# A selective scan in units of one channel chunk by four states, with B's product on TensorE and GpSimd for the last image

## The chip, the cores and the metric

The kernel runs on one core of a Trainium2 chip. Its engines are called by the names of the profile: PE (TensorE), DVE (VectorE), ACT (ScalarE), POOL (GpSimd) and SP (SyncE, which issues most DMAs here). The metric is the device time of one execution in microseconds (us); lower is better. Before the change the median of three runs was 25,891.06 us (25,885.81 to 25,894.32).

## The reference

Two layers work on x of shape (4, 128, 128, 128): four images of 128 x 128 pixels and 128 channels, all float32. Each layer adds its result to its input, after a group norm.

- Layer 0 is a deformable convolution in two groups of 64 channels. A convolution gives an offset for each of nine taps; at each displaced place the input is sampled bilinearly from four neighbours; a depthwise 3 x 3 convolution and a 1 x 1 convolution follow.
- Layer 1 takes each image row as four rows of 128 tokens in blocks, and runs two Mamba blocks over them. The heart of a block, per channel d (256 of them) and state n (16):

```python
deltaA = jnp.exp(jnp.einsum('btd,dn->btdn', delta, A))
deltaBu = jnp.einsum('btd,btn->btdn', delta * u, Bm)
...
    h = dA * h + dBu
    y = jnp.einsum('bdn,bn->bd', h, c)
```

delta comes from a softplus, B and C from a projection of u, and after the scan `y + u * Dp` is multiplied by silu(res) and projected. The group norm of layer 1 takes statistics over a whole image of layer 0's result, so layer 1 of an image begins when layer 0 of it is done.

## The kernel before

Layer 0 of image 0 runs alone. Then layer 1 of image b runs beside layer 0 of image b + 1, and layer 1 of the last image runs alone. The two are written as Python generators, `layer0` and `layer1`, and the loop at the end of `block_kernel` (L732 to L745) takes steps of each in turn: 512 steps of layer 1 for an image, and 289 of layer 0, of which the last falls 24 steps before the image's end. The framework places instructions on the engines' queues and makes all waits; each engine runs its queue in order.

Layer 0, by step: `gather` (L347) issues eight indirect DMAs from POOL's queue, of 128 rows each, into two of four `gt` buffers; that is, two steps are in flight. `sample` (L368) multiplies them by the bilinear weights, the first half in one DVE product (`gw`, L387), the second in sixteen ACT instructions (L382), PE transposes the sums into PSUM, and ACT copies them into one of NSB = 4 buffers `s` (L401). `add_up` (L404) applies the combined convolutions on PE. `table_part` (L207) builds the table that is gathered from: it loads four rows and one more into `xt` (two buffers), normalizes them into `xg` (one buffer) and writes eight DMAs of 64 KB. All tables are built before layer 1 starts.

Layer 1, by job: a job is one block of four image rows (TB = 512 tokens, SR = 4 sequences of 128) in one of the two Mamba layers; there are 64 jobs for an image. `pre` (L511) makes u, the gate g, delta, B and C of the next job, in pieces between the units of the job before it: a projection with u on PE, softplus from Abs, Relu, Exp and Ln on ACT and three DVE operations (L588 to L590), and `du` = delta * u (L591). B and C are written to DRAM (`bcd`) and read back, broadcast to 128 partitions.

`main` (L598) has eight units for a job. A unit covers both channel chunks (NC = 2, 128 channels each) and NQ = 2 states: a tile of 128 x 2,048.

- Loads of B and of C, 512 KB each, two buffers of each (L617).
- ACT: a zero copy into the first column of each sequence (L622) and four exponentials (L627) into one of three `da` buffers.
- DVE, images 0 to 2: two products du * B of 128 x 1,024 into `hs` (L661), one scan over 2,048 (L667), one product with C (L670). The products are `scalar_tensor_tensor` with a column of ones.
- DVE, last image: four scans of 512 that read B's product from PSUM (L653), and one `tensor_tensor` with C (L656). B's product is made from a transposed du (`turn_du`, L496): xs = dut * B, for one state of the two on POOL (L646), for the other on ACT (L644), then PE transposes it back into PSUM (L651).
- PE adds the sixteen transposed 128 x 128 blocks into `y` (L674, in the helper at L128). `y` is opened by the products with D (L606).

After eight units y is multiplied by the gate (L677), transposed, projected, and either becomes the next layer's input or is written out (L676 to L702).

Of the kernel before, what the change touches and what calls it, by code (L numbers as in the profile page):

```python
# [31 lines left out]
XP = DTR + 1 + 2 * NS  # L32

# [30 lines left out]
def block_kernel(ctx: ExitStack, tc: tile.TileContext, a: dict, out: bass.AP):  # L64
# [26 lines left out]
    pb = ctx.enter_context(tc.tile_pool(name="l0b", bufs=1))  # L91
    ps = ctx.enter_context(tc.tile_pool(name="l0ps", bufs=2, space=PSUM))
    psa = ctx.enter_context(tc.tile_pool(name="l0psa", bufs=2, space=PSUM))
# [3 lines left out]
    psy = ctx.enter_context(tc.tile_pool(name="l1psy", bufs=1, space=PSUM))  # L97

# [6 lines left out]
    offw = loadw("offw", [P, NT, 64])  # L105
# [10 lines left out]
    ones = cw.tile([P, P], F32, name="ones")  # L116
    nc.vector.memset(ones, 1.0)

    wc = cw.tile([P, NT, NT, CG], F32, name="wc")
# [43 lines left out]
    cvw = loadw("cvw", [P, NL, DCONV, NC * P], pool=p2, tag="hs")  # L163
# [7 lines left out]
    xn = cw.tile([P, RB + 2, WP], F32, name="xn")  # L171
    nc.vector.memset(xn, 0.0)

    NSB = 4
    sbuf_s = [cw.tile([P, 4, WP], F32, name=f"s{i}") for i in range(NSB)]
# [5 lines left out]
    def stats_part(b, j):  # L181
        if j == 0:
            stats[b] = small.tile([P, NJ, 6], F32, tag="stats", name=f"stats_{b}")
        xr = pb.tile([P, 4, P], F32, tag="xr", name=f"xr_{b}_{j}", bufs=2)
        nc.sync.dma_start(xr, x[b, 4 * j : 4 * j + 4].rearrange("r w c -> w r c"))
        pt4 = ps.tile([P, 4, P], F32, tag="t", name=f"pt4_{b}_{j}")
        for i in range(4):
            nc.tensor.transpose(pt4[:, i, :], xr[:, i, :], ident)
        nc.vector.bn_stats(stats[b][:, j, :], pt4.rearrange("p r w -> p (r w)"))

    def norm_part(b):
# [3 lines left out]
        for nm, v in (("s", scale), ("b", bias)):  # L195
# [4 lines left out]
            row = small.tile([P, P], F32, tag=f"row_{nm}", name=f"row_{nm}_{b}")  # L200
# [6 lines left out]
    def table_part(b, j):  # L207
# [4 lines left out]
        xt = pb.tile([P, 5, P], F32, tag="xt", name=f"xt_{b}_{j}", bufs=2)  # L212
# [4 lines left out]
        xg = pb.tile([P, G, 5, CG], F32, tag="xg", name=f"xg_{b}_{j}", bufs=1)  # L217
# [248 lines left out]

    NDA = 3
    das = [cw.tile([P, NC, NQ, SR, P], F32, name=f"da{i}") for i in range(NDA)]
    zero = cw.tile([P, NC * NQ * SR], F32, name="zero")
    nc.vector.memset(zero, 0.0)  # L470
    n_da = [0]

# [20 lines left out]
    duts = []  # L493
    n_dut = [0]

    def turn_du(st, nm):  # L496

        if not duts:
            duts.append(p2.tile([P, 2, SR, NC * P], F32, tag="hs", name="duts"))
        n_dut[0] += 1  # L500
        dut = duts[0][:, n_dut[0] % 2]
        for k in range(SR // 2):
            pt = ps1.tile([P, 2, NC, P], F32, tag="t", name=f"pdu_{nm}_{k}")
            for i in range(2):
                for c in range(NC):
                    o = (2 * k + i) * P
                    nc.tensor.transpose(pt[:, i, c, :], st["du"][:, c, o : o + P], ident)
            nc.scalar.copy(dut[:, 2 * k : 2 * k + 2], pt.rearrange("p s c d -> p s (c d)"))  # L508
        st["dut"] = dut

    def pre(st, l):  # L511

        blk = st["blk"]
        nm = f"{blk}_{l}"
# [45 lines left out]
        if in_last(blk):  # L560

            pbt = ps1.tile([P, SR, XP], F32, tag="t", name=f"pbt_{nm}")
            for i in range(SR):
                nc.tensor.transpose(pbt[:, i, :], dbl[:, i * P : (i + 1) * P], ident[0:XP, 0:XP])
            st["bt"] = p2.tile([P, SR, NS], F32, tag="bt", name=f"bt_{nm}", bufs=2)
            nc.scalar.copy(st["bt"], pbt[:, :, DTR + 1 : DTR + 1 + NS])
# [4 lines left out]
        du = p2.tile([P, NC, TB], F32, tag="du", name=f"du_{nm}", bufs=2)  # L571
# [11 lines left out]
        nc.scalar.activation(du, w1, AF.Ln)  # L583
        nc.scalar.activation(w1, w1, AF.Identity, bias=-1.0)
# [3 lines left out]
        nc.vector.tensor_tensor(e, w1, e, ALU.subtract)  # L588
        nc.vector.tensor_tensor(de, de, e, ALU.subtract)
        nc.vector.tensor_tensor(de, de, du, ALU.add)  # L590
        nc.vector.tensor_tensor(du, de, u, ALU.mult)  # L591
        st.update(u=u, g=g, delta=de, du=du, bcd=bcd)
        st.pop("dut", None)
        if in_last(blk) and duts:
            yield
            turn_du(st, nm)

    def main(st, l):  # L598

        blk = st["blk"]  # L600
        nm = f"{blk}_{l}"

        y = psy.tile([P, SR, NC, P], F32, tag="y", name=f"y_{nm}")
# [6 lines left out]
        if in_last(blk) and "dut" not in st:  # L610
            turn_du(st, nm)
        for q in range(NS // NQ):
            bc = []
            for w in range(in_last(blk), 2):
                t = p2.tile([P, NQ, TB], F32, tag=f"bc{w}", name=f"bc{w}_{nm}_{q}", bufs=2)
                n0 = w * NS + q * NQ
                nc.sync.dma_start(t, st["bcd"][n0 : n0 + NQ, :].partition_broadcast(P))  # L617
                bc.append(t)
            da = das[n_da[0] % NDA]
            n_da[0] += 1  # L620

            nc.scalar.copy(da.rearrange("p c n s t -> p (c n s) t")[:, :, 0], zero)  # L622
            for c in range(NC):
                dv = st["delta"][:, c].rearrange("p (s t) -> p s t", s=SR)
                for n in range(NQ):
                    s = q * NQ + n
                    nc.scalar.activation(  # L627
                        da[:, c, n, :, 1:], dv[:, :, 1:], AF.Exp, scale=aneg[:, l, c, s : s + 1]
                    )
            dc = da.rearrange("p c n s t -> p c (n s t)")  # L630
            cv = bc[-1].rearrange("p n t -> p (n t)").unsqueeze(1).to_broadcast([P, NC, NQ * TB])
            if in_last(blk):


                for n in range(NQ):
                    s = q * NQ + n

                    xs = (p2 if n else pb).tile(
                        [P, SR, NC * P], F32, tag="bc0" if n else "gw", name=f"xs_{nm}_{s}", bufs=2
                    )  # L640
                    for i in range(SR):
                        bv = st["bt"][:, i, s : s + 1]
                        if n:
                            nc.scalar.activation(xs[:, i], st["dut"][:, i], AF.Copy, scale=bv)  # L644
                        else:
                            nc.gpsimd.tensor_scalar(xs[:, i], st["dut"][:, i], bv, None, ALU.mult)  # L646
                    for c in range(NC):
                        pool, tag = (ps, "t") if n else (psa, "acc")
                        px = pool.tile([P, SR, P], F32, tag=tag, name=f"px_{nm}_{s}_{c}")
                        for i in range(SR):  # L650
                            nc.tensor.transpose(px[:, i, :], xs[:, i, c * P : (c + 1) * P], ident)  # L651
                        dn = da[:, c, n].rearrange("p s t -> p (s t)")
                        nc.vector.tensor_tensor_scan(  # L653
# [57 lines left out]
    def layer1():  # L711
        for _ in pre(*jobs[0]):
            pass
# [30 lines left out]
    for _ in l1:  # L744
        pass  # L745
# [77 lines left out]
```

## Time and profile before

The profiled execution has a span of 24,903.2 us from the first to the last instruction, with a mean granted PE clock of 0.905. Its own time is known by this span alone; the median of the runs is 987.9 us above it.

| Stage (us from the span's start) | length | PE busy | DVE busy | ACT busy | POOL busy | DMA share | GB/s |
|---|---|---|---|---|---|---|---|
| 0 to 275: statistics and table of image 0 | 275 | 55 | 98 | 7 | 1 | 0.51 | 147 |
| 275 to 3,344: layer 0 of image 0, other tables | 3,069 | 2,494 | 686 | 1,373 | 2,335 | 0.50 | 144 |
| 3,344 to 20,567: layer 1 of images 0 to 2, layer 0 of 1 to 3 | 17,223 | 13,966 | 16,346 | 11,257 | 13,270 | 0.48 | 156 |
| 20,567 to 24,903: layer 1 of the last image | 4,337 | 3,471 | 3,805 | 3,471 | 2,350 | 0.21 | 69 |

Busy times are in us. In the page's groups of instructions, a line names the code line, the engine, the operation, the tiles written and read, their shapes and the count; then the busy time of the group and the mean of one in ns; then the idle time of the engine just before these instructions and what ended most of it. In a timeline, a line is a start and a length in us, the engine, line, operation and tiles, and in brackets the idle time before. A line of waits names who waited, for whom, the sum in us, how often, and the longest.

Of rows that the diff touches: the scan of 2,048 (L667) takes 4,422 ns, the product of 2,048 with C 2,350 ns (L670, scalar_tensor_tensor) or 2,289 ns (L656, tensor_tensor), a scan of 512 from PSUM 1,202 ns, an exponential 711 ns on ACT, and one xs on POOL 1,164 ns on average.

### The profile page before, as it was taken

The numbers are of one execution on the slowest core, as the hardware profiler recorded it, in microseconds if no ns is written. First come the engines' busy times: TensorE is split into PE (matmuls) and PEld (weight loads), VectorE is DVE, ScalarE is ACT, GpSimd is POOL, SyncE is SP. The second block draws the span as 40 slices with busy tenths as digits, with TensorE's granted clock in tenths as the row PEclk, the third lists the DMA queues.
The fourth block names the chain that finished last, engine by engine and source line by source line (L and its number), as shares of the span: only waits on it lengthen the run. The fifth ranks groups of instructions, "written<-read, shape, count | busy, mean of one in ns | idle before, by whom it ended". The sixth has DMA issues, their size and how long they took to land. (4 is left out here: it accounts for less than half of the span.)

```text
span 24903.2 us, 331178 instructions
## 1 busy us (share of the span) xinstructions
PE 19986.7 (80%) x121156; PEld 13946.7 (56%) x121156; DVE 20935.3 (84%) x13018; ACT 16107.7 (65%) x38037; POOL 17956.4 (72%) x11270
## 2 busy tenths in 40 slices
PE   5788788888888878888888878888888877878877
PEld 3555455555555555555555555555555556666666
DVE  2221269999999999999999999999999998888888
ACT  2444466666666666666666666666666667888887
POOL 4777777887887857788887866787887845555555
PEclk8999989999999888999999888999999889999999
DMA  4554544454444444454544444454454442222221
GB/s 136 157 159 130 151 142 157 156 161 158 158 159 156 158 145 153 157 162 157 159 161 155 159 150 151 153 163 158 159 160 157 157 138 67 69 69 71 70 69 68
DMA packets 1530815, 3471.82 MB, mean 139 GB/s; under 512 B 243283, under 2 KB 717651, under 8 KB 1529052
## 3 DMA queue, kind: packets, MB, share of 16 engines
q1 hardware_dynamic: 1086812, 2242.08, 28.0%
q0 software_dynamic: 442368, 1208.55, 15.4%
q8 instruction: 951, 15.58, 0.3%
q14 instruction: 684, 5.60, 0.1%
HBM read 3299.19 MB, written 150.47 MB: 139 GB/s over the span
## 5 line engine op out<-in xcount | busy, mean ns | idle before, releaser
L359 POOL DMA_INDIRECT gt<-table,idx x9216 | 15606.0, 1693 | 4665.8 <-issue 2582.2
L627 ACT ACTIVATE da<-de,aneg 128x508 f32<-128x508 f32 x8192 | 5455.4, 711 | 2609.2 <-PE y L128 2357.7
L667 DVE TENSOR_TENSOR_SCAN da<-da,hs 128x2048 f32<-128x2048 f32 x1536 | 6792.2, 4422 | 120.2 <-ACT da L627 23.8
L128 PE MATMUL y<-ident,da 128*128 128x128 f32 x32768 | 4753.9, 306 | 2176.1 <-DVE da L670 1901.2
L420 PE MATMUL acc<-s,wc 128*64 128x256 f32 (+3 forms) x38400 | 6060.3, 439 | 276.7 <-ACT s L401 269.1
L128 PEld LDWEIGHTS y<-ident,da 128*128 128x128 f32 x32768 | 4247.0, 159 | 2997.4 <-DVE da L670 2050.8
L382 ACT ACTIVATE gw<-gt,wt 128x64 f32<-128x64 f32 x18432 | 4613.2, 337 | 1024.2 <-DMA gt<-table,idx 592.1
L420 PEld LDWEIGHTS acc<-s,wc 128*64 128x64 f32 x38400 | 3200.8, 140 | 2440.1 <-issue 1287.5
L128 PE MATMUL p<-ident,gw 128*128 128x128 f32 x18432 | 2896.6, 305 | 1471.5 <-DVE gw L387 1215.5
L646 POOL TENSOR_SCALAR xs<-duts,bt 128x256 f32<-128x256 f32 x2048 | 2349.7, 1164 | 2249.2 <-ACT duts L508 1185.7
L661 DVE SCALAR_TENSOR_TENSOR hs<-du,ones,bc 128x1024 f32<-128x1024 f32 x3072 | 3828.0, 1281 | 0.0
L670 DVE SCALAR_TENSOR_TENSOR da<-da,ones,bc 128x2048 f32<-128x2048 f32 x1536 | 3609.6, 2350 | 31.8
L128 PEld LDWEIGHTS p<-ident,gw 128*128 128x128 f32 x18432 | 2363.9, 157 | 2272.0 <-DVE gw L387 1150.1
L387 DVE TENSOR_TENSOR gw<-gt,wt 128x1024 f32<-128x1024 f32 x1152 | 1403.7, 1219 | 2357.9 <-DMA gt<-table,idx 1883.7
L653 DVE TENSOR_TENSOR_SCAN da<-da,px 128x512 f32<-128x512 f32 x2048 | 2350.6, 1202 | 509.2 <-PE px L651 509.2
L401 ACT COPY s<-p 128x512 f32<-128x512 f32 x1152 | 669.7, 581 | 2102.5 <-PE p L128 2100.1
L530 PE MATMUL pu<-hp,inc 128*128 128x512 f32 x4096 | 1830.4, 594 | 1.1 <-ACT ot L700 0.8
L651 PE MATMUL px<-ident,xs 128*128 128x128 f32 x8192 | 1213.5, 287 | 537.8 <-DVE da L653 322.1
L651 PEld LDWEIGHTS px<-ident,xs 128*128 128x128 f32 x8192 | 972.2, 147 | 818.0 <-POOL xs L646 329.3
L530 PEld LDWEIGHTS pu<-hp,inc 128*128 128x128 f32 x4096 | 747.8, 190 | 813.1 <-issue 809.3
L656 DVE TENSOR_TENSOR da<-da,bc 128x2048 f32<-128x2048 f32 x512 | 1172.0, 2289 | 6.6
L644 ACT ACTIVATE xs<-duts,bt 128x256 f32<-128x256 f32 x2048 | 894.3, 499 | 19.3 <-PE px L651 18.8
(133 smaller groups left out, 14768.7 us busy)
## 6 DMA issues: line engine op xcount, KB each, us to landing
bc<-bcd SPq DMA_DIRECT2D x3584, 512.0 KB
gt<-table,idx POOLq DMA_INDIRECT x9216
table<-xg SPq DMA_DIRECT2D x1016, 64.0 KB
xt<-in_x SPq DMA_DIRECT2D x124, 320.0 KB
xr<-in_x SPq DMA_DIRECT2D x128, 256.0 KB
x<-xo SPq DMA_DIRECT2D x128, 256.0 KB
x1t<-x SPq DMA_DIRECT2D x128, 256.0 KB
x1t_o<-x SPq DMA_DIRECT2D x128, 256.0 KB
```

Source lines behind the costliest of these rows:

```text
L128: nc.tensor.matmul(o, v, ident, is_transpose=True, start=start, stop=stop, skip_group_check=True)
L359: nc.gpsimd.indirect_dma_start(out=gt[:, v, r], out_offset=None, in_=flat, in_offset=bass.IndirectOffsetOnAxis(ap=idx[:, ri, o : o + 1], a ...
L382: nc.scalar.activation(gw[:, r, s, v], gts[h][:, v, r, s * CG : (s + 1) * CG], AF.Copy, scale=wt[:, u, r0 + r, s, v : v + 1],)
L420: nc.tensor.matmul(accs[b, j + i0][CG * g : CG * g + CG, q : q + rb - ra, :], wc[sl, v, e, :], st[p + 4 * g if p < 4 else 8][sl, ra:rb, kx ...
L530: nc.tensor.matmul(px.rearrange("p (s t) -> p s t", s=SR), inc[:, l, j, c * P : (c + 1) * P], h[:, :, j : j + P], start=(j == 0), stop=(j ...
L627: nc.scalar.activation(da[:, c, n, :, 1:], dv[:, :, 1:], AF.Exp, scale=aneg[:, l, c, s : s + 1])
L646: nc.gpsimd.tensor_scalar(xs[:, i], st["dut"][:, i], bv, None, ALU.mult)
L651: nc.tensor.transpose(px[:, i, :], xs[:, i, c * P : (c + 1) * P], ident)
L653: nc.vector.tensor_tensor_scan(dn, dn, px.rearrange("p s t -> p (s t)"), 0.0, ALU.mult, ALU.add)
L661: nc.vector.scalar_tensor_tensor(hs[:, :, n, :], st["du"], ones[:, 0:1], bc[0][:, n].unsqueeze(1).to_broadcast([P, NC, TB]), op0=ALU.mult, ...
L667: nc.vector.tensor_tensor_scan(df, df, hs.rearrange("p c n t -> p (c n t)"), 0.0, ALU.mult, ALU.add)
L670: nc.vector.scalar_tensor_tensor(dc, dc, ones[:, 0:1], cv, op0=ALU.mult, op1=ALU.mult)
```

## The change

A unit is now one channel chunk by NU = 4 states, still 128 x 2,048, and there are still eight for a job. In all images B's product of a unit has one source:

- Images 0 to 2: one DVE product of 2,048 (du of the chunk, broadcast over the states, times B), one scan, one product with C. B and C of four states, 1 MB each, are loaded every second unit. `du` has one buffer and is made during the last unit of the job before.
- Last image, chunk 0: du is transposed in a permuted order, so that 32 tokens of each of four groups lie on 32 partitions. `make_d` (POOL) spreads B over a 32-column mask, and `fill` makes the product B * du on PE in sixteen matmuls of 32 rows, straight into a PSUM tile of four banks.
- Last image, chunk 1: `times_b` multiplies du by the broadcast B on POOL, 128 x 2,048.
- Last image: the exponentials of a unit are issued two units ahead, into four `da` buffers whose first columns are zeroed once; the scan writes into its own `he` buffers (three).
- Layer 0's tiles lie in pools of their own, which are released before the last image; those used only while image 0 is alone, in one released before layer 1. `xt` has four buffers, `xg` two, `s` three (NSB).
- The softplus: w1 - 1 - e is one scalar_tensor_tensor; an ACT instruction falls away.

```diff
+QW = P // SR
+NU = 4
...
-    NSB = 4
-    sbuf_s = [cw.tile([P, 4, WP], F32, name=f"s{i}") for i in range(NSB)]
+    NSB = 3
+    sbuf_s = [l0w.tile([P, 4, WP], F32, name=f"s{i}") for i in range(NSB)]
...
-        xt = pb.tile([P, 5, P], F32, tag="xt", name=f"xt_{b}_{j}", bufs=2)
+        xt = pp.tile([P, 5, P], F32, tag="xt", name=f"xt_{b}_{j}", bufs=4)
...
-        xg = pb.tile([P, G, 5, CG], F32, tag="xg", name=f"xg_{b}_{j}", bufs=1)
+        xg = pp.tile([P, G, 5, CG], F32, tag="xg", name=f"xg_{b}_{j}", bufs=2)
...
+    def load_bc(st, u):
+
+        bc = []
+        for w in range(2):
+            t = lm["pool"].tile([P, NU, TB], F32, tag=f"bc{w}", name=f"bc{w}_{st['nm']}_{u}", bufs=2)
+            n0 = w * NS + u * NU
+            nc.sync.dma_start(t, st["bcd"][n0 : n0 + NU, :].partition_broadcast(P))
+            bc.append(t)
+        st["bc", u] = bc
...
-        nc.scalar.activation(w1, w1, AF.Identity, bias=-1.0)
...
-        nc.vector.tensor_tensor(e, w1, e, ALU.subtract)
+        nc.vector.scalar_tensor_tensor(e, w1, -1.0, e, op0=ALU.add, op1=ALU.subtract)
...
+    def make_du(st):
+
+        du = p2.tile([P, NC, TB], F32, tag="du", name=f"du_{st['nm']}")
+        nc.vector.tensor_tensor(du, st["delta"], st["u"], ALU.mult)
+        st["du"] = du
...
+    def main(st, l, nst, nl):
...
+        for k in range(NC * NS // NU):
+            u, c = divmod(k, NC)
+            if c == 0:
+                load_bc(st, u)
+            bt, ct = (t.rearrange("p n t -> p (n t)") for t in st["bc", u])
...
+            hs = lm["pool"].tile([P, NU, TB], F32, tag="hs", name=f"hs_{nm}_{k}")
+            nc.vector.scalar_tensor_tensor(
+                hs, st["du"][:, c].unsqueeze(1).to_broadcast([P, NU, TB]), one, st["bc", u][0],
+                op0=ALU.mult, op1=ALU.mult,
+            )
+            if k == NC * NS // NU - 1 and nst and not in_last(nst["blk"]):
+                make_du(nst)
+            df = da.rearrange("p n s t -> p (n s t)")
+            nc.vector.tensor_tensor_scan(df, df, hs.rearrange("p n t -> p (n t)"), 0.0, ALU.mult, ALU.add)
+            nc.vector.scalar_tensor_tensor(df, df, one, ct, op0=ALU.mult, op1=ALU.mult)
...
-                for n in range(NQ):
-                    nc.vector.scalar_tensor_tensor(
-                        hs[:, :, n, :], st["du"], ones[:, 0:1],
-                        bc[0][:, n].unsqueeze(1).to_broadcast([P, NC, TB]),
-                        op0=ALU.mult, op1=ALU.mult,
-                    )
...
+    def make_d(st, u):
+
+        d = le["r"].tile([P, SR, NU, QW], F32, tag="D", name=f"D_{st['nm']}_{u}", bufs=3)
+        nc.gpsimd.tensor_tensor(
+            d, st["bt"][:, :, NU * u : NU * u + NU].unsqueeze(3).to_broadcast([P, SR, NU, QW]),
+            le["mask"].unsqueeze(1).unsqueeze(1).to_broadcast([P, SR, NU, QW]), ALU.mult,
+        )
+        st["D", u] = d
+
+    def fill(st, u):
+
+        px = le["ps"].tile([P, SR, NU, P], F32, tag="dbu", name=f"px_{st['nm']}_{u}")
+        for q in range(SR):
+            for g in range(SR):
+                o = slice(g * QW, (g + 1) * QW)
+                nc.tensor.matmul(
+                    px[:, g, :, q * QW : (q + 1) * QW],
+                    st["dut"][o, q], st["D", u][o, q],
+                    start=True, stop=True, skip_group_check=True,
+                )
+        st["px"] = px
+
+    def times_b(st, u):
+
+        t = le["r"].tile([P, SR, NU, P], F32, tag="dbu", name=f"dbu_{st['nm']}_{u}", bufs=2)
+        nc.gpsimd.tensor_tensor(
+            t, st["du1"].rearrange("p (s t) -> p s t", s=SR).unsqueeze(2).to_broadcast([P, SR, NU, P]),
+            st["bc", u][0].rearrange("p n (s t) -> p s n t", s=SR), ALU.mult,
+        )
+        st["dbu", u] = t
+
+    def main_last(st, l, nst, nl):
...
+        for k in range(nk):
+            u, c = divmod(k, NC)
+            nxt = (st, u + 1) if k + 2 < nk else (nst, 0)
+            if nxt[0]:
+                if c == 0:
+                    load_bc(*nxt)
+                    if k + 2 < nk:
+                        make_d(*nxt)
+                else:
+                    times_b(*nxt)
+            if k + 2 < nk:
+                exps(st, l, k + 2)
+            elif nst:
+                exps(nst, nl, k + 2 - nk)
+            hs = le["r"].tile([P, SR, NU, P], F32, tag="he", name=f"he_{nm}_{k}", bufs=3)
+            src = st.pop(("dbu", u)) if c else st["px"]
+            nc.vector.tensor_tensor_scan(
+                hs.rearrange("p s n t -> p (s n t)"),
+                st.pop(("da", k)).rearrange("p s n t -> p (s n t)"),
+                src.rearrange("p s n t -> p (s n t)"), 0.0, ALU.mult, ALU.add,
+            )
+            if c == 0 and nxt[0]:
+                fill(*nxt)
+            nc.vector.tensor_tensor(
+                hs, hs, st["bc", u][1].rearrange("p n (s t) -> p s n t", s=SR), ALU.mult
+            )
```

## The prediction

> **What bounds the kernel now.** I read the 40 slices first, then the groups by line, then the timelines of VectorE (DVE) and GpSimd (POOL) side by side, then the waits. The slices show three stages: a start without scans (to 3,344 us), 1,536 scan units of images 0 to 2 beside the gathers (to 20,567 us), and the last image without gathers (4,337 us).
>
> ```profile
> DVE  2221269999999999999999999999999998888888
> POOL 4777777887887857788887866787887845555555
> ...
> L359 POOL DMA_INDIRECT gt<-table,idx x9216 | 15606.0, 1693 | 4665.8 <-issue 2582.2
> L667 DVE TENSOR_TENSOR_SCAN da<-da,hs 128x2048 f32<-128x2048 f32 x1536 | 6792.2, 4422 | 120.2 <-ACT da L627 23.8
> L661 DVE SCALAR_TENSOR_TENSOR hs<-du,ones,bc 128x1024 f32<-128x1024 f32 x3072 | 3828.0, 1281 | 0.0
> L670 DVE SCALAR_TENSOR_TENSOR da<-da,ones,bc 128x2048 f32<-128x2048 f32 x1536 | 3609.6, 2350 | 31.8
> ```
>
> In the middle DVE is busy 16,346 of 17,223 us: it sets the pace, and 565 us of its idle time are waits of gw (L387) for gathered rows. POOL, which only issues gathers there, looks like a cover (13,270 us busy). One plain unit shows how thin that cover is:
>
> ```profile
> 12083.29 4.42 DVE L667 TENSOR_TENSOR_SCAN da<-da,hs 128x2048 f32<-128x2048 f32 x1
> 12087.75 2.35 DVE L670 SCALAR_TENSOR_TENSOR da<-da,ones,bc 128x2048 f32<-128x2048 f32 x1
> 12090.02 2.48 DVE L661 SCALAR_TENSOR_TENSOR hs<-du,ones,bc 128x1024 f32<-128x1024 f32 x2
> 12092.60 4.42 DVE L667 TENSOR_TENSOR_SCAN da<-da,hs 128x2048 f32<-128x2048 f32 x1
> ```
>
> ```profile
> 12084.42 4.05 POOL L359 DMA_INDIRECT gt<-table,idx  x1 [0.30 <-ACT da L627]
> 12088.78 2.15 POOL L359 DMA_INDIRECT gt<-table,idx  x1 [0.31 <-issue]
> 12091.23 0.95 POOL L359 DMA_INDIRECT gt<-table,idx  x1 [0.30 <-issue]
> 12092.48 0.95 POOL L359 DMA_INDIRECT gt<-table,idx  x1 [0.30 <-issue]
> ```
>
> A gather takes 0.95 us if it finds DVE between two operations. Issued inside the scan it ends 0.76 us after the scan does (12,088.47 against 12,087.71); issued inside the C product, 0.83 us after that. So a DVE operation with two SBUF inputs holds POOL's read until it ends, and POOL gets in at each boundary. This unit of 9.31 us has four: after the scan, after the C product, between the two hs products, and after the second.
>
> POOL's own waits in the steady part (4,000 to 20,400 us) are its whole reserve:
>
> ```profile
> POOL gt L359 <- DVE gw L387: 1144.2, 151, 112.1
> POOL gt L359 <- ACT gw L382: 376.9, 94, 27.1
> ```
>
> With smaller ones they come to 1,590 us; the rest of the 16,400 us is 6,609 gathers at 1.93 us and 0.3 us of issue.
>
> The last image runs at 4,337 / 64 = 67.8 us a job (one block, one layer, eight units); DVE is busy 3,805 / 64 = 59.5 us of it. Its large wait is L653 for px, 509 us in all, where POOL, ScalarE and TensorE pass xs on.
>
> ```profile
> 22566.71 2.29 DVE L656 TENSOR_TENSOR da<-da,bc 128x2048 f32<-128x2048 f32 x1
> 22568.92 4.55 DVE L653 TENSOR_TENSOR_SCAN da<-da,px 128x512 f32<-128x512 f32 x4
> ```
>
> ```profile
> 22563.30 3.62 POOL L646 TENSOR_SCALAR xs<-duts,bt 128x256 f32<-128x256 f32 x4 [11.69 <-PE px L651]
> 22567.15 5.34 POOL L646 TENSOR_SCALAR xs<-duts,bt 128x256 f32<-128x256 f32 x4 [0.23 <-PE px L651]
> ```
>
> Beside scans that read PSUM, four xs take 3.62 us (0.92 us each alone, counted over 1,300); those that meet the two-input C product take 5.34.
>
> **Start.** xg gets two buffers, xt four. A table step takes 5.7 us now; DVE waits for the table writes before refilling xg (91.9 us in 30 waits until 340 us). SP's own issue of a step is 8 x 0.455 + 0.43 = 4.1 us, the next limit: 30 x 1.6 = -48 us. If the transfers bind, 0. Afterwards POOL is 76% busy and 22% issuing (2,335 and 668 of 3,069 us): nothing more to win.
>
> **Middle, DVE.** Two hs products of 1,024 become one of 2,048. Their pair spans 2.48 us; a 2,048 product (L670) takes 2.35: -0.13 us a unit, at most -0.20 if the 0.12 us before the scan shrinks to the 0.04 us that stand between scan and product. 1,536 x 0.13 = -200 us (-130 to -310). Scan, C product, exponentials, transposes and loaded bytes per unit stay. du is multiplied later, once as before; e as scalar_tensor_tensor costs 256 x 0.06 = 16 us, inside the rounding.
>
> **Middle, POOL.** This is where I choose. The boundary between the two hs products disappears. A gather started 1.1 us after the C product now waits for the end of hs, ends 0.82 us later, and the next starts about 1 us into the scan: three gathers in 9.2 us (3.07 us each) instead of four in 9.31. Counted in the instruction records of the steady part, 1,087 gathers got their read at this boundary; so many must be fitted elsewhere. POOL's 1,590 us hold 1,590 / 3.07 = 518 of them, if every wait can be used. The other 569 run only while DVE stands idle, at 0.95 + 0.30 = 1.25 us: +711 us, entered as gw waiting for its gather. Gaps at image changes (up to 112 us) can't be used, so I take +750. Upper bound 1,150: most of the waits remain. Lower bound 350: half of the losses are recovered at the ends of other operations (gw, softplus and g products) or fall where POOL has time.
>
> In sentences apart: the Trainium skill, "SBUF — State Buffer" (Who interferes with whom), says that a DVE instruction with two SBUF inputs and a GpSimd instruction that reads SBUF exclude each other for the whole instruction, whichever is first. The 4.05 and 0.95 us rows agree for short POOL reads, and it speaks against making DVE instructions longer here. By the busy shares alone the middle would be -200 us; by rows and rule it is +550.
>
> **Last image, DVE.** Four 512 scans (4.58 us) and a C product (2.21 from start to next start) become one 2,048 scan (4.46, as L667) and the same product: 13.34 us for the chunk 0 and chunk 1 units. Four pairs are 53.4; softplus, du and g products (some five of 1.2 us) add 5.9: 59.3 us. Exponentials and the first px are made a unit or more ahead; I leave 1 us of waits: 60.3 us, -480 us over 64 jobs.
>
> **Last image, POOL.** New rows: times_b, 2,048 elements from two SBUF inputs, and make_d, 512, once a pair. Near rows: in xs, a C product begun 0.22 us after it lasted 2.39 instead of 2.27 us, one begun 0.44 us after was not lengthened. So 256 elements of one input are read within 0.2 to 0.34 us; two inputs in turn give 3.2 to 5.4 us for times_b and 0.8 to 1.36 for make_d. times_b waits for the chunk 1 scan that frees its buffer, is held by that unit's C product, then reads beside the chunk 0 scan, which has one SBUF input: 4.46 us hide it. make_d, queued behind times_b, comes next, at the end of the C product, and holds up the chunk 1 scan. I take 4.2 us (hidden) and 1.05 us (paid): 4.2 us a job, so 64.5 us, -210 us (-480 without any holding; +110 at 5.4 and 1.36). If the whole 0.92 us scaled with length (7.35 and 1.84), 4.7 us a pair are paid: +730.
>
> "GPSIMD Engine Reference" (Performance versus the Vector engine) gives 4,497 ns for a 2,048-element fp32 tensor_tensor; with that the sum is the same. No run here shows it yet.
>
> **Other waits.** px has one buffer: fill waits for the chunk 0 scan, TensorE's y transposes queue behind it; 16 small matmuls, priced by L606's 0.13 us spacing at 2 to 4 us, have 9 us until the next chunk 0 scan. B and C loads double to 1 MB every second unit: a C load waits on SP two units ahead, the gather stage's loads queue behind it, and DVE has some 18 us before it needs it. In the last image the rate goes from 69 to about 140 GB/s, below the middle's 156. Three s buffers: TensorE's own order has used the first pair before the third's copy; were it not so, 864 copies of 0.58 us would be 500 us. ScalarE loses xs and the zero copies there. All at nothing.
>
> **Sum.** -48 - 200 + 750 - 210 = +292 us. Made on the profiled span: 24,903 + 292 = 25,195. Of what lies around the span I only know that the median is 988 us above it; I keep that: 25,891 + 292 = 26,183, taken as 26,180 us (1.1% slower). If that part scaled, it would change by 12 us.
>
> **Rivals.**
> - POOL's reserve is enough (faster): its 24% idle and issue time speaks for it, DVE's existing gw waits and the three-in-9.2 count against. Then -48 - 200 - 210: 25,433 us.
> - The gathers bind, but DVE is not held in the last image: -48 + 550 - 480 = +22: 25,913 us. The lengthened 2.39 us products speak against.
> - times_b reads longer than the chunk 0 scan (from 4.46 us on), at the whole xs price: 25,891 - 48 + 550 + 730 = 27,123 us. The short read found in xs speaks against.
>
> **Numbers.** Forecast 0.60, rivals 0.22, 0.11, 0.07. The forecast's own range is 25,700 to 26,650; with 8 in 10 it reaches down to the first rival: 25,430 to 26,650. About 0.2% (52 us) can be told from no change: faster 0.25 (the first rival, and a little of the second), same 0.07, slower 0.68.
>
> **What would show it.** Gathers of the plain middle units: three a unit, their mean up from 1.93 towards 2.3 us; gw's waits up from 565 to some 1,300 us and POOL's waits for gw nearly gone; the middle some 550 us longer. In the last image a job near 64.5 us, make_d ending about 1 us after a C product and the scan behind it late. I am wrong if gathers still go four to a unit, or if gw's waits stay: then the first rival holds.

## The result and the profile after

| | before | after |
|---|---|---|
| median of the timed runs, us | 25,892.69 (25,885.81 to 25,933.18, 4 runs) | 26,847.44 (26,817.57 to 26,882.69, 4 runs) |
| ratio | | 1.0367, 95% interval 1.0353 to 1.0382 |
| profiled span, us | 24,903.2 | 26,880.9 |
| start, to the first main scan | 3,344 | 4,304 |
| middle, to the end of the last main scan | 17,218 | 17,976 |
| last image | 4,341 | 4,600 |

The change costs 955 us, 3.7%. The forecast had the sign, and 1.1%; the time lies outside its range of 25,700 to 26,650 us.

The two spans can't be subtracted: 960 of their 1,978 us lie in the start. The first experiment shows that this part is not the change's. What is the change's stands in the two other stages: +758 and +259 us.

From the page of the changed kernel, the two slices that were shown of before (busy tenths of VectorE and GpSimd) and the groups that answer to those of before (line, engine, operation; busy us and mean ns; idle time ahead of them and what ended most of it):

```profile
DVE  2211115889888889988998899988899899999998
POOL 3555557888888886888888886888888864444444
...
L365 POOL DMA_INDIRECT gt<-table,idx x9216 | 17443.0, 1893 | 4550.8 <-issue 2639.4
L696 DVE TENSOR_TENSOR_SCAN da<-da,hs 128x2048 f32<-128x2048 f32 x1536 | 6792.1, 4422 | 303.8 <-ACT da L687 174.4
L697 DVE SCALAR_TENSOR_TENSOR da<-da,one,bc 128x2048 f32<-128x2048 f32 x1536 | 3614.7, 2353 | 34.1
L689 DVE SCALAR_TENSOR_TENSOR hs<-du,one,bc 128x2048 f32<-128x2048 f32 x1536 | 3614.5, 2353 | 0.0
L740 POOL TENSOR_TENSOR dbu<-du,bc 128x2048 f32<-128x2048 f32 x256 | 1420.8, 5562 | 1713.7 <-issue 944.5
L778 DVE TENSOR_TENSOR he<-he,bc 128x2048 f32<-128x2048 f32 x512 | 1565.1, 3076 | 2.2
```

VectorE's product with B is cheaper, as meant: 3,614.5 us where two products were 3,828.0. In the middle many of VectorE's nines have become eights all the same: it is busy 16,162 of 17,976 us, against 16,343 of 17,218. It does 181 us less and stands idle 939 us more. The gathers became longer, 1,893 ns on average from 1,693, and VectorE's C product of the last image lasts 3,076 ns where it lasted 2,289.

A plain stretch of the middle like the one shown of before, first VectorE, then GpSimd, in the changed kernel (start, duration, engine, line, operation):

```profile
12102.14 4.42 DVE L696 TENSOR_TENSOR_SCAN da<-da,hs 128x2048 f32<-128x2048 f32 x1
12106.60 2.35 DVE L697 SCALAR_TENSOR_TENSOR da<-da,one,bc 128x2048 f32<-128x2048 f32 x1
12108.87 2.35 DVE L689 SCALAR_TENSOR_TENSOR hs<-du,one,bc 128x2048 f32<-128x2048 f32 x1
12111.32 4.42 DVE L696 TENSOR_TENSOR_SCAN da<-da,hs 128x2048 f32<-128x2048 f32 x1
```

```profile
12103.23 4.09 POOL L365 DMA_INDIRECT gt<-table,idx  x1 [0.30 <-issue]
12107.63 2.15 POOL L365 DMA_INDIRECT gt<-table,idx  x1 [0.30 <-issue]
12110.08 1.96 POOL L365 DMA_INDIRECT gt<-table,idx  x1 [0.30 <-issue]
12112.34 4.16 POOL L365 DMA_INDIRECT gt<-table,idx  x1 [0.30 <-issue]
```

Three gathers to a unit, each ending after a VectorE operation has ended: 12,107.32 after the scan (12,106.56), 12,109.78 after the C product (12,108.95), 12,112.04 after the product with B (12,111.22). Between 5,000 and 20,000 us there are 456 units that take less than 10 us from one scan's start to the next, and so hold no other large operation of VectorE; in 438 of them exactly three gathers begin (mean 2.91). In the kernel before there are 533, and four gathers begin in 448 of them (mean 3.60). These plain units are counted in the same way below. The price of the lost gather, in the waits of the middle of the changed kernel (us in total, times, longest):

```profile
DVE gw L393 <- DMA gt<-table,idx: 1101.5, 244, 10.2
DVE da L696 <- ACT da L687: 174.4, 67, 9.1
...
POOL gt L365 <- DVE gw L393: 462.6, 58, 94.5
```

gw waits 1,102 us for gathered rows (565 before), and GpSimd's own waits for gw, its reserve, fell to 463 us. In the middle of the kernel before, as profiled in experiment 1, they were:

```profile
POOL gt L359 <- DVE gw L387: 1216.7, 165, 112.1
```

The last image, VectorE, GpSimd and TensorE in one stretch of the changed kernel:

```profile
24024.68 4.41 DVE L771 TENSOR_TENSOR_SCAN he<-da,px 128x2048 f32<-128x2048 f32 x1
24029.01 4.42 DVE L771 TENSOR_TENSOR_SCAN he<-da,dbu 128x2048 f32<-128x2048 f32 x1
24033.35 8.79 DVE L778 TENSOR_TENSOR he<-he,bc 128x2048 f32<-128x2048 f32 x2
24045.26 4.42 DVE L771 TENSOR_TENSOR_SCAN he<-dae,px 128x2048 f32<-128x2048 f32 x1 [3.13 <-PE px L730]
```

```profile
24033.51 6.48 POOL L740 TENSOR_TENSOR dbu<-du,bc 128x2048 f32<-128x2048 f32 x1 [4.37 <-DVE he L771]
```

```profile
24036.24 2.03 PE L579 MATMUL pr<-w_resw,hp 128*128 128x256 f32 x4 [2.17 <-ACT u L574]
24038.19 1.22 PE L730 MATMUL px<-D,dut 32*128 32x128 f32 x12
24041.49 2.08 PE L579 MATMUL pr<-w_resw,hp 128*128 128x256 f32 x4 [2.07 <-ACT u L574]
24043.49 1.65 PE L730 MATMUL px<-D,dut 32*128 32x128 f32 x20
```

Here VectorE does not run scan, C, scan, C, as the code has it: it does both scans of the pair and then both C products. So it goes in 129 of the 256 pairs, two in each job. GpSimd's product (times_b), freed at the end of the chunk 1 scan, waits through the first C product (2.26 us in the instruction records), takes its turn at the boundary, and the second C product, issued at 24,035.53, lasts 6.60 us in place of 2.28. In one of the two pairs of each job a C product is held like that, 64 times, 276 us in all. In the other, both C products last some 3.1 us beside make_d; 161 C products are held so, 127 us in all, and 34 chunk 1 scans last 5.26 us in place of 4.41, 29 us. Then VectorE waits 3.13 us for px, whose filling TensorE has in two pieces behind the residual products (pr) of the next job, and these wait for ScalarE. The second C product ends at 24,042.14 and the filling at 24,045.14: the hold and the filling run side by side, and the filling is the later by 3 us.

### The profile page after: what moved, and what is told of

Same layout as the page of the kernel before. It is cut to its first block, busy times and chain, and to the rows that moved or that the text cites. A ratio compares the mean times of both kernels' runs of the same rounds, so it can differ in the third digit from the quotient of the medians.

```text
span 26880.9 us, 317133 instructions
## 1 busy us (share of the span) xinstructions
PE 20386.5 (76%) x120900; PEld 13857.4 (52%) x120900; DVE 21108.1 (79%) x10014; ACT 14999.2 (56%) x35223; POOL 19595.9 (73%) x9734
## 4 chain that ended last, share of the span: by engine, by line
POOL 32%; issue 21%; DVE 17%; PE 15%; ACT 7%; DMA 4%; another core or an unknown queue 3%; SPq 0%; DVEq 0%; ACTq 0%; POOLq 0%
POOL gt L365 32%; PE acc L426 6%; DVE he L771 5%; DMA gt<-table,idx 4%; DVE da L696 4%; PE p L134 2%; DVE da L697 2%; ACT gw L388 2%; DVE hs L689 2%; PE y L134 2%; DVE he L778 2%; ACT da L687 1%; DVE gw L393 1%; PE pr L579 1%
## 5 line engine op out<-in xcount | busy, mean ns | idle before, releaser
L365 POOL DMA_INDIRECT gt<-table,idx x9216 | 17443.0, 1893 | 4550.8 <-issue 2639.4
L687 ACT ACTIVATE da<-de,aneg 128x508 f32<-128x508 f32 x6144 | 4081.1, 711 | 1449.8 <-PE y L134 1373.9
L134 PE MATMUL y<-ident,da 128*128 128x128 f32 x24576 | 3591.6, 306 | 1591.6 <-DVE da L697 1570.5
L134 PEld LDWEIGHTS y<-ident,da 128*128 128x128 f32 x24576 | 3197.5, 159 | 2342.3 <-DVE da L697 1721.1
L697 DVE SCALAR_TENSOR_TENSOR da<-da,one,bc 128x2048 f32<-128x2048 f32 x1536 | 3614.7, 2353 | 34.1
L689 DVE SCALAR_TENSOR_TENSOR hs<-du,one,bc 128x2048 f32<-128x2048 f32 x1536 | 3614.5, 2353 | 0.0
L740 POOL TENSOR_TENSOR dbu<-du,bc 128x2048 f32<-128x2048 f32 x256 | 1420.8, 5562 | 1713.7 <-issue 944.5
L134 PE MATMUL y<-ident,he 128*128 128x128 f32 x8192 | 1369.0, 334 | 797.9 <-DVE he L778 797.9
L134 PEld LDWEIGHTS y<-ident,he 128*128 128x128 f32 x8192 | 1209.1, 176 | 971.9 <-DVE he L778 851.5
L778 DVE TENSOR_TENSOR he<-he,bc 128x2048 f32<-128x2048 f32 x512 | 1565.1, 3076 | 2.2
```

Of the source, the lines that this page charges most:

```text
L134: nc.tensor.matmul(o, v, ident, is_transpose=True, start=start, stop=stop, skip_group_check=True)
L365: nc.gpsimd.indirect_dma_start(out=gt[:, v, r], out_offset=None, in_=flat, in_offset=bass.IndirectOffsetOnAxis(ap=idx[:, ri, o : o + 1], a ...
L687: nc.scalar.activation(da[:, i, :, 1:], dv[:, :, 1:], AF.Exp, scale=aneg[:, l, c, n : n + 1])
L689: nc.vector.scalar_tensor_tensor(hs, st["du"][:, c].unsqueeze(1).to_broadcast([P, NU, TB]), one, st["bc", u][0], op0=ALU.mult, op1=ALU.mult,)
L697: nc.vector.scalar_tensor_tensor(df, df, one, ct, op0=ALU.mult, op1=ALU.mult)
L740: nc.gpsimd.tensor_tensor(t, st["du1"].rearrange("p (s t) -> p s t", s=SR).unsqueeze(2).to_broadcast([P, SR, NU, P]), st["bc", u][0].rearr ...
```

## The experiments

Edits are against the changed kernel unless said otherwise. Stages are read as above; the two figures of the changed kernel to compare with are 17,976 us (middle) and 4,600 us (last image).

**1. The kernel before, profiled again.** No edit.

> The kernel before, unchanged, profiled a second time, because its first profile (span 24,903 us) lies 988 us under the median of its timed runs (25,891), while the changed kernel's profile (span 26,881) lies at its timed runs. Between the two profiles the start (up to the first 2,048-element scan of the main loop) went from 3,344 to 4,304 us, the middle from 17,223 to 17,981, the last image from 4,321 to 4,594. Theory A: the start of the kernel before also takes about 4,300 us in most of its executions, and the first profile caught a short one: span about 25,890, start about 4,330, middle 17,220 and last image 4,320 as before. Then the changed kernel's loss is 758 + 273, less some 30 to 70 at the start. Theory B: the start is 3,344 us in every execution, and the 988 us lie in the middle or the last image of the timed runs: span about 25,890 with the start at 3,344; then the changed kernel has lost 960 us in the start by itself and won elsewhere.

Span 25,822.5 us: start 4,257, middle 17,224, last image 4,341. Theory A holds. Runs 2 to 4, made together with this one, show the same start (4,256, 4,218 and 4,213 us), and the seven runs made in two later groups (5 to 8 and 9 to 11), all of edited versions of the changed kernel, have 3,303 to 3,319 us, while the timed median of the kernel before was 25,808 us in the first group and 24,911 and 24,891 in the later ones. So the start takes one of two lengths some 900 us apart, the same for all runs made together, in both kernels alike; why, these runs don't show. Within the first group the start of the edited versions of the changed kernel is 39 to 44 us shorter than before's.

**2. One product with B in the kernel before.**

```diff
-                for n in range(NQ):
-                    nc.vector.scalar_tensor_tensor(
-                        hs[:, :, n, :], st["du"], ones[:, 0:1],
-                        bc[0][:, n].unsqueeze(1).to_broadcast([P, NC, TB]),
-                        op0=ALU.mult, op1=ALU.mult,
-                    )
+                nc.vector.tensor_tensor(
+                    hs, st["du"].unsqueeze(2).to_broadcast([P, NC, NQ, TB]),
+                    bc[0].unsqueeze(1).to_broadcast([P, NC, NQ, TB]), ALU.mult,
+                )
```

> The kernel before with the product with B of the main loop as one tensor_tensor of 2,048 elements for both states and chunks, instead of two of 1,024; all else as it was, the last image too. Theory A (the boundary between the two products let a fourth gather of each unit read its indices): VectorE's own work in the middle falls by some 150 to 230 us, the mean gather rises from 1.93 to 2.1 to 2.3 us, and the middle grows from 17,223 us to between 17,700 and 18,100. Rival (the loss in the middle comes with something else of the change: the loads of 8 KB a partition, three s buffers in place of four, the units of one chunk): the middle stays at 17,223 or falls, down to 17,000, with the mean gather within 0.1 us of 1.93.

Ratio 1.037 (1.0350 to 1.0391): this one edit costs as much as the whole change. Middle 18,153 us, VectorE busy 16,067 (277 less, where 150 to 230 were expected) and idle 2,086 (1,206 more); 2.92 gathers to a plain unit; mean gather 2.21 us. Theory A; the middle grew by 50 us more than its upper bound. The last image is unchanged at 4,341.

**3. The product with B cut in two in the changed kernel.**

```diff
-            nc.vector.scalar_tensor_tensor(
-                hs, st["du"][:, c].unsqueeze(1).to_broadcast([P, NU, TB]), one, st["bc", u][0],
-                op0=ALU.mult, op1=ALU.mult,
-            )
+            for i in range(0, NU, 2):
+                nc.vector.scalar_tensor_tensor(
+                    hs[:, i : i + 2], st["du"][:, c].unsqueeze(1).to_broadcast([P, 2, TB]), one,
+                    st["bc", u][0][:, i : i + 2], op0=ALU.mult, op1=ALU.mult,
+                )
```

> The changed kernel with the main loop's product with B cut into two instructions of 1,024 elements, two states each; the units, the loads, the buffers and the last image stay as changed. Theory A (the missing boundary): the mean gather falls from 2.17 to about 1.9 us, the middle from 17,981 us to between 17,000 and 17,350, and the whole by 600 to 950 us, to 25,900 to 26,250. Rival (other parts of the change hold the middle): the two products cost 2.48 us in place of 2.35, which is some 200 us more of VectorE's work over 1,536 units, and the middle stays within 200 us of 17,981.

Ratio 1.0022 (1.0012 to 1.0031), where the changed kernel has 1.0367. Middle 17,026 us, 3.78 gathers to a plain unit, last image 4,597. VectorE does 180 us more and idles 1,129 us less. VectorE's largest wait in the middle of this kernel, against the 1,101.5 above:

```profile
DVE gw L393 <- DMA gt<-table,idx: 286.6, 84, 7.7
```

So the missing boundary holds the whole loss of the middle, and the rest of the change had won 198 us there (17,224 to 17,026, at the same busy time of VectorE). Which part of it won them was not tried.

**4. and 5. The hold in the last image.** In the first attempt a one-element copy on GpSimd read the end of the C product ahead of times_b, but into a tile of its own; in the second it writes into the tile that times_b then fills. The second edit:

```diff
-                else:
-                    times_b(*nxt)
...
+            if c and nxt[0]:
+                times_b(*nxt, hs[:, SR - 1, NU - 1, P - 1 :])
...
+        if gate is not None:
+            nc.gpsimd.tensor_copy(t[:, SR - 1, NU - 1, P - 1 :], gate)
```

> The changed kernel with GpSimd's product with B of the last image (chunk 1) issued behind a one-element GpSimd copy that reads the end of the C product of chunk 1, so that it starts beside the next scan of chunk 0, which reads PSUM, and not as soon as the scan that frees its buffer ends. In the changed kernel 64 C products of the last image, one a job, last 6.6 us where others last 2.28, and 129 of the 327 GpSimd products last 6.5: one such pair in each job. Theory A (GpSimd's product gets hold in a boundary between two VectorE operations with two SBUF inputs, and keeps the second one waiting for its whole length): no C product above 4 us is left, GpSimd's product is down to about 4.5 us, 276 us of VectorE's time come free, and the last image falls from 4,594 us to 4,300 to 4,450; the C products of 3.08 us, 151 of them, beside the small product with the mask, stay. Rival (the 6.6 us are a wait that moves, as the next scan of chunk 1 then waits for the product instead): the last image stays within 80 us of 4,594 or grows.

Ratio 1.0364 (1.0347 to 1.0381), last image 4,596 us, and C products of 6.60 us are still there (one begins at 24,033.29): nothing bound the copy to the product, which was put elsewhere in GpSimd's order. The run tells nothing about either theory.

> The changed kernel with the hold of the C product in the last image truly taken away: the one-element GpSimd copy now writes into the tile that GpSimd's product then fills, so that the product can't start before the C product of chunk 1 has ended (in the run before, the copy wrote elsewhere, the product was scheduled ahead of it, and the 6.6 us stayed). Last image of the changed kernel: 4,600 us; in each job VectorE does scan px, scan dbu, C, C for the units of the second pair, the second C lasts 6.6 us, and 3.1 us later the next scan of px begins, when TensorE has filled px. Theory A (the hold is on the path): 64 C products back to about 2.3 us and the last image 4,310 to 4,400. Theory B (TensorE's fill of px stands behind the next job's residual product, which waits for ScalarE, and px would come no earlier): the last image stays within 80 us of 4,600, and VectorE's idle time ahead of the px scans grows from 420 us to about 700.

Now no C product is longer than 3.2 us and VectorE is busy 247 us less in the last image (3,917 us), but the stage is no shorter: 4,670 us. Ratio 1.0404 (1.0383 to 1.0425). Theory B. Waits of VectorE for px in the last image, first of the changed kernel, then of this one:

```profile
DVE he L771 <- PE px L730: 388.3, 116, 3.9
```

```profile
DVE he L771 <- PE px L730: 669.4, 116, 7.5
```

The 4.3 us of holding have become 4.4 us of waiting, 64 times (the longest wait goes from 3.9 to 7.5 us): px was late anyway.

**6. px filled first.**

```diff
-                if last and k in (1, 3):
+                if last and k in (2, 3):
```

> The changed kernel with one step of the next job's preparation (its Silu, its residual product) called after unit 2 of the last image's jobs and not after unit 1, so that TensorE's fill of px for that unit stands ahead of the residual product in its queue. The hold by GpSimd stays. Theory B (fill behind a product that waits for ScalarE): the 3.1 us ahead of that scan go, 64 times, so the last image falls from 4,600 by 150 to 220 us. Theory A (the hold alone): it stays within 80 us. If what moves later in ScalarE's order (the exponentials behind the Silu) becomes late instead, the last image grows.

Last image 4,401 us (199 less), with 64 C products of 6.6 us still there; VectorE's wait for px falls to half:

```profile
DVE he L771 <- PE px L730: 207.5, 56, 3.9
```

Theory B again. Ratio 1.0297 (1.0276 to 1.0318).

**7. Two products, gate and fill first.** The edits of 3, 5 and 6 together.

> Three edits together: two products with B of 1,024 in the main loop, the GpSimd product of the last image behind the C product, and the fill of px ahead of the residual product. Middle as with two products before, 17,026 us (16,980 to 17,080). Last image, if the hold (4.3 us a job) and the wait for px (3.1 us a job) stand in a row on one path: 4,600 less 64 x 7.4 = 470, so about 4,130 (4,080 to 4,250); if each only hides the other: 4,310 to 4,400. The whole against the kernel before: 0.985 or 0.993.

Ratio 0.9872 (0.9856 to 0.9888). Middle 17,046, last image 4,230 us. The gate (the copy ahead of times_b) is worth 171 us with px filled first (4,401 to 4,230); alone it was worth nothing. So the two don't stand one behind the other, as the expectation put it: they run side by side, the filling of px ends later, and the hold counts only once px is early. Together they give 370 of the some 470 us that the expectation named; where the missing 100 went stays open.

**8. Four products, and VectorE's order kept.**

```diff
+            for i in range(0, NU, 1):
...
+            with tc.issue_after(le["c"].ins) if "c" in le else ExitStack():
+                nc.vector.tensor_tensor_scan(
...
-            nc.vector.tensor_tensor(
+            le["c"] = nc.vector.tensor_tensor(
                 hs, hs, st["bc", u][1].rearrange("p n (s t) -> p s n t", s=SR), ALU.mult
```

with the edit of 6; no gate.

> Middle: the product with B in four instructions of 512 elements, one state each. Theory A by numbers of boundaries (one product 17,976 us, two 17,026): two more boundaries between VectorE operations with two SBUF inputs, but VectorE's idle time is only 685 us with two products, and four products add some 2 x 0.06 us of VectorE to 1,536 units, about 200 us; so the middle is 16,900 to 17,250, with the mean gather below 1.97. Last image: the fill first as in the run beside it, and VectorE kept to scan, C, scan, C in every unit, so that a GpSimd product freed by the end of a scan of chunk 1 waits through one C product and then runs beside the px scan, as the forecast had assumed: no C product of 6.6 us, last image 4,080 to 4,350.

Middle 17,756 us: the expectation missed by 500. A product of 512 lasts 746 ns on average, four of them 2.73 us from the first's start to the last's end, and VectorE is busy 394 us more than with two and idle 335 us more. No more gathers come of it: 3.55 to a plain unit (3.78 with two). In one unit, VectorE and GpSimd:

```profile
11440.07 2.73 DVE L690 SCALAR_TENSOR_TENSOR hs<-du,one,bc 128x512 f32<-128x512 f32 x4
```

```profile
11430.96 7.55 POOL L365 DMA_INDIRECT gt<-table,idx  x1 [0.30 <-issue]
11441.28 1.02 POOL L365 DMA_INDIRECT gt<-table,idx  x1 [0.30 <-issue]
11442.60 1.02 POOL L365 DMA_INDIRECT gt<-table,idx  x1 [0.30 <-issue]
```

Beside the four products the gathers end 1.32 us apart, a gather and its issue, while the products begin 0.66 us apart: only every second end is used. And some gathers let ends pass: the one of 7.55 us began under the last product of the unit before and ended only 0.74 us after the next scan, with gw and du between. Between 5,000 and 20,000 us 239 gathers last longer than 5.3 us, where run 9, with two products, has 38; why they miss the ends, the runs don't show. Last image 4,098 us, a job 64.06 us, as expected. Ratio 1.0105 (1.0088 to 1.0122).

**9. Two products, VectorE's order kept, fill first.** The edits of 3, 6 and the order of 8.

> Two products with B of 1,024 elements in the main loop (middle 17,026 and 17,046 us in two runs), and in the last image VectorE kept to scan, C, scan, C with the fill of px ahead of the residual product (4,098 us in the run with four products). If the two stages are independent: middle 17,000 to 17,060, last image 4,080 to 4,120, so some 130 us under the run with the gate (0.9872 of the kernel before), 0.981 to 0.983. Rival (the last image's 4,098 came with the lighter gathers at the end of the four-product middle): last image above 4,180, 0.986 or more.

Ratio 0.9819 (0.9803 to 0.9835): 24,437.6 us against 24,890.7 of the kernel before beside it. Middle 17,028, last image 4,097. This version beats both kernels. Its last image, VectorE and GpSimd:

```profile
22025.26 2.29 DVE L780 TENSOR_TENSOR he<-he,bc 128x2048 f32<-128x2048 f32 x1
22027.47 4.41 DVE L773 TENSOR_TENSOR_SCAN he<-dae,px 128x2048 f32<-128x2048 f32 x1
22031.92 2.29 DVE L780 TENSOR_TENSOR he<-he,bc 128x2048 f32<-128x2048 f32 x1
```

```profile
22025.31 6.61 POOL L741 TENSOR_TENSOR dbu<-du,bc 128x2048 f32<-128x2048 f32 x1 [6.67 <-DVE he L773]
```

times_b, freed at the start of a C product, waits through it and then runs beside the scan that reads PSUM; it ends at 22,031.92, 0.04 us after that scan, and nothing on VectorE is longer for it. Why keeping the order is worth 133 us more than the gate of run 7 stays open.

**10. The C product cut instead.** One product with B; the order of 8 without the edit of 6.

```diff
-            nc.vector.scalar_tensor_tensor(df, df, one, ct, op0=ALU.mult, op1=ALU.mult)
+            for i in (slice(0, 2 * TB), slice(2 * TB, 4 * TB)):
+                nc.vector.scalar_tensor_tensor(df[:, i], df[:, i], one, ct[:, i], op0=ALU.mult, op1=ALU.mult)
```

> Middle: one product with B of 2,048 as in the changed kernel, but the C product of the main loop in two instructions of 1,024. If what counts is how many boundaries between two-input VectorE operations a unit has, wherever they are: middle 17,000 to 17,100, like two products with B. If the boundary must lie ahead of the scan: 17,900 to 18,200. Last image: VectorE kept to scan, C, scan, C, but the fill of px still behind the residual product. If the order alone would have made the forecast true: about 4,100. If the fill is a second, separate condition: 4,300 to 4,450, since the hold of 4.3 us goes and the wait of 3 us a job stays or grows.

Middle 16,917 us, 83 below the band, 3.77 gathers to a plain unit: a boundary in the C product does what one in the product with B does, and is 110 us better. The last image is 4,482 us, 32 above its band: the order alone is not enough, the fill is a second condition (idle 606 us, against 262 in run 9). Ratio 0.9927 (0.9907 to 0.9947).

**11. A short operation in place of a cut.** One product with B, with the last image of run 9.

```diff
+            with tc.issue_after(h.ins):
+                h = nc.vector.memset(gap, 0.0)
+            with tc.issue_after(h.ins):
+                nc.vector.tensor_tensor_scan(df, df, hs.rearrange("p n t -> p (n t)"), 0.0, ALU.mult, ALU.add)
```

> Middle: one product with B as in the changed kernel, and between it and the scan a memset of one element, which reads no SBUF input; 1,536 of them at some 0.06 us are 90 us of VectorE. If GpSimd's read gets in whenever a two-input operation has ended, and what counts is how many such ends a unit has with the port free, the memset makes one boundary into two and lets a second gather in: middle 17,100 to 17,500. If a boundary lets one gather in however long it is, because a second gather comes too late for it: middle 17,950 to 18,150. Last image as in the run with order and fill first: 4,080 to 4,120.

Middle 17,834 us, 2.92 gathers to a plain unit. 1,536 memsets of 59 ns let no further gather in; 17,834 is a little below the band named for this outcome. Two boundaries 0.06 us apart are one, for GpSimd. Ratio 1.0141 (1.0121 to 1.0162), last image 4,100.

The cut C product and the last image of run 9 were not run together. From their stages 24,432 - (17,028 - 16,917) = 24,321 us of span, an estimate.

## Why the forecast had the direction and not the size

Point by point, in us:

| step | forecast | measured |
|---|---|---|
| start | -48 | -39 to -44 (runs 1 to 4) |
| middle, VectorE | -200 | -181 |
| middle, GpSimd | +750 (350 to 1,150) | +939 as idle time of VectorE |
| last image | -210 (-480 to +110) | +259 |
| sum | +292 | about +975 by stages, +955 timed |

The forecast missed by some 680 us as the stages add up: 469 in the last image, 208 in the middle.

**Start.** The size came out, the place only in part. GpSimd's wait for the first table was to end 48 us sooner; it went from 273 to 276 us down to 248 to 250, some 25 us. Up to 340 us VectorE's waits for table writes fell from 91.9 to 39.4 us, but those for x rose from 24.6 to 58.4. Where the rest of the gain lies stays open. What lies "around the span" was not around it: the first profile of before came from an execution with the short start, the timed runs had the long one. The 988 us were rightly left as they were.

**Middle.** The mechanism was right in all its signs: three gathers a plain unit, a mean gather of 2.20 us, gw's waits at 1,102 us where 1,300 were named. The size was low. Counted against the version with two products, the boundary is worth 1,129 us of idle time, close to the upper bound, of which the rest of the change gave 198 back. The step "POOL's 1,590 us hold 1,590 / 3.07 = 518 of them, if every wait can be used" gave the reserve too much: 463 us of waits for gw are left, one of them 94.5 us long, and the late gathers delayed more than gw (the scan's wait for ScalarE's exponentials rose to 174 us). The rival with enough reserve is refuted by runs 2 and 3.

**Last image.** Here the forecast failed, at two steps. "times_b waits for the chunk 1 scan that frees its buffer, is held by that unit's C product, then reads beside the chunk 0 scan": this takes for granted that VectorE does scan, C, scan, C. In two of the four pairs of each job it did scan, scan, C, C, and in one of them the product that should be hidden held a C product for 4.3 us. And px at nothing ("have 9 us until the next chunk 0 scan"): TensorE's queue had the next job's residual products between the pieces of the fill, and these wait for ScalarE; 3.1 us a job. Taken away alone, the hold gives nothing (run 5) and the late fill 199 us (run 6). With both conditions made true the job takes 64.05 us (run 9), where the forecast's sum was 64.5. That they lie so close is in part luck. The duration of times_b was good, if short: 4.2 us entered, 4.5 to 4.6 measured for 126 of the 256 in the changed kernel (the others, some 6.5, include the C product that they wait through). But make_d, at 1.05 us paid per pair, cost less (in the changed kernel 156 us in all, 2.4 us a job of the 4.2 entered; in run 9 94 us, 1.5 a job), and VectorE's waits in run 9 are 262 / 64 = 4.1 us a job, where 1 us was left for them. That also refutes the rival in which times_b costs seven; the one in which VectorE is not held at all fell with the 6.60 us. The order in which VectorE's operations would run was taken from the code, which has scan, C, scan, C; the trace shows another, which the framework made.

The Trainium skill, "SBUF — State Buffer" (Who interferes with whom), states that a two-input VectorE instruction and a GpSimd instruction reading SBUF exclude each other for the whole instruction, whichever is first. Both halves are seen here: gathers of 4.09 us behind a scan, and a C product of 6.60 us behind times_b.

## What to carry to other kernels

Before two operations of the engine that sets the pace are merged, count who else gets in at the boundary between them: 0.12 us of work saved a unit (181 / 1,536) brought 0.61 us of idle time (939 / 1,536) here, and one cut, at either of two places in the unit, brings the gathers back. A cut into four pieces of 0.75 us, shorter than a gather with its issue (1.25 us), brought no further gather and cost 730 us against two. An operation moved to another engine is hidden only if the queues really have the order that the sum assumes; price it in both orders, and where it matters write the order out. Where a hold and a wait run side by side, removing the one that ends sooner shows nothing (run 5), and removing the later one shows no more than the difference (run 6): try both together before calling either harmless.

## What the runs showed that was not expected

- A VectorE operation can be held for all of a long GpSimd operation: 6.60 us for a product of 2.28, in each of 64 jobs.
- Cutting one product of 2,048 costs VectorE's time with each cut: 2.35 us in one piece, 2.48 in two, 2.73 in four, about 0.13 us a cut. Four pieces are not 4 x 0.75 us, since one begins before the one ahead of it has ended.
- A gather that waits does not always get in at the next end of a VectorE operation: with four products over 200 gathers let one or more pass (run 8).
- The start of both kernels, with no scans in it, has two lengths, by the group of runs, 3,303 to 3,319 and 4,213 to 4,304 us in the changed kernel and its edits, 3,344 and 4,257 in the kernel before. In the long one (both of the kernel before) GpSimd is busy 58% and not 76% of the time between 1,000 and 3,000 us, and the granted clock of TensorE is 0.84 and not 0.91; which is cause and which effect stays open. A comparison between a profile of one group and times of another would be off by 900 us.
